# Four attention blocks on one core: a PSUM tile, the order of GpSimd's sums, first loads and products, and the order of the last outputs

## The chip, the cores and the metric

The kernel runs on one core of a Trainium2 chip. The metric is the device time of one execution in microseconds, the median of several runs. In the profile PE is TensorE (matmuls), PEld its weight loads, DVE VectorE, ACT ScalarE, POOL GpSimd, and SP the engine whose queue issues all DMAs here. L716 is line 716 of the kernel before.

## The reference

Four images, `x` of shape (4, 512, 32, 32) in float32, go through four layers, each of which adds its result to `x`. Seen as 512 channels by 1024 positions:

```python
# layer 0: attention, 8 heads of 64
attn = softmax(q @ k.T * 64**-0.5);  x = attn @ v @ Wo.T + bo + x
# layer 1: linear attention with softplus features of 64, and a gate
V = (max(x) + mean(x)) * (wv @ x + bv);  KV = softplus(K) @ V.T
x = x + gamma * (softplus(Q) @ KV) / (softplus(Q) @ sum(softplus(K)))
# layer 2: layer norm over channels, attention with one head of 512
x = x + (softmax(q @ k.T * 512**-0.5) @ v) @ w_proj.T + b_proj
# layer 3: group norm (32 groups), attention, 4 heads of 128
x = x + proj(softmax(q @ k.T * 128**-0.5) @ v)
```

In layers 0, 2 and 3 q, k and v are products of the (normed) input with one weight matrix.

## The kernel before

Everything is in float32. A product of 512 columns goes to PE as two matmul instructions of 0.43 us each, one of 256 columns as two of 0.216.

**Seven products instead of eight.** A product of a 2 by 2 block matrix of weights with a 2 by 2 block matrix of inputs is done with seven block products rather than eight (a Strassen scheme in Winograd's form): in `seven_products` for the projections and the scores of layer 2, in `project_out` for the output projections, in `one_head` for the values of layer 2. Each needs four sums of weight blocks and four of input blocks. `sum_weights` (L702) makes the weight sums on POOL: s[0] (L704), s[1] from s[0] (L705), s[2] (L706), s[3] from s[1] (L707). `sum_inputs` (L692) makes the input sums on DVE. The products are called p1 to p7: p6 takes s[1], p7 s[2], p5 s[0], p3 s[3]. In `seven_products` p1 and p2 of a pair of blocks come first, which need no sums, then p6, p7, p6, p5, p4, p7, p3, p5, p4, p3.

**Order.** PE's order is the order in which the program traces its matmuls (`manual_schedule` for PE). On the other engines a scheduler orders the whole program when it is compiled: among the instructions whose operands it believes to be ready it prefers the one traced earlier. `tc.issue_after(i)` puts what its block traces on i's engine behind i on that engine; it is an order, not a wait. All engines then run in order.

**Where the sums are traced.** In layers 0 and 3 `project_qkv` (L871) calls `seven_products` for four blocks of q and k, with one `sum_weights` each through `block_sums`, then `project_v` (L853), which makes its own four sums once for both of its blocks (L857) into a tile `ws`. In layer 2 the loop over the images b = 0 to 3 traces, in this order: `seven_products` for q with two `sum_weights` (L801); `sum_weights(places, ...)` of the finished q, in the profile `qs`, for the scores (L815); `project_v` with its sums of `hv` (in the profile `ws<-w`, L831 and L857); `one_head` (L832), whose scores take the sums of q. `hv` is made before the loop, q in each turn of it.

**Output projections.** `project_out` (L1071) adds seven products to `x` for one half of the positions (`qb`) of an image in layers 0 and 3. It returns three parts, `second`, `third` and `fourth`, that are called later from the list `later`: after some turns of the attention loop, or all at once. Its first product p1 goes to a PSUM tile ps[1], ACT copies it to `d` (L1112), and `second` adds the second product to the same PSUM tile (`start=False`). `acc_tile` has four buffers in all, for these and for the values and the row sums of attention. The last half of the last image is projected by `end_program` (L1135) without the scheme: three of four chunks of each of four outputs, then `end()` (the verdict: a check whether the fast path held, which ends in `count`), then the last chunk of outputs 0, 2, 1, 3. Outputs 0 and 1 share a PSUM tile, and so do 2 and 3. `finish` (L1065) adds each on DVE and stores it.

**Start.** SP's queue loads chunk by chunk the first half of the positions of image 0 and the q weights (L587, L588), then the k weights (L591), the second half of `x` (L592), the v weights (L593). The first `seven_products` (`first=True`) runs p1 and p2 chunk by chunk for all four blocks, then takes the sums: DVE's need the second half of `x`, POOL's the k weights and the q weights.

## Time and profile before

| what | time |
|---|---|
| median of 3 runs | 2415.14 us (2414.91 to 2416.72) |
| the profiled execution, its own time | 2416.26 us |
| its span, first to last instruction | 2414.5 us |
| PE busy | 2398.0 us, 99% |
| DVE, ACT, POOL busy | 1503.3, 702.0 and 247.8 us |
| share of the chain that ended last | PE 97%, DVE 2% |

Where the four layers lie in the span, read from the groups by line: layer 0 with layer 1 interleaved from the start to about 960 us, layer 2 to 1566 us, layer 3 from there. A row of a timeline gives start and duration, engine, line, operation, output<-inputs, shape and count, and in brackets how long the engine was idle before and what ended that. A row of waits gives the engine and what it made, what it waited for, the total in us, the times and the longest.

### The profile page before, as it was taken

The numbers are of one execution on the slowest core, as the hardware profiler recorded it, in microseconds if no ns is written. First come the engines' busy times: TensorE is split into PE (matmuls) and PEld (weight loads), VectorE is DVE, ScalarE is ACT, GpSimd is POOL, SyncE is SP. The second block draws the span as 40 slices with busy tenths as digits, with TensorE's granted clock in tenths as the row PEclk, the third lists the DMA queues.
The fourth block names the chain that finished last, engine by engine and source line by source line (L and its number), as shares of the span: only waits on it lengthen the run. The fifth ranks groups of instructions, "written<-read, shape, count | busy, mean of one in ns | idle before, by whom it ended". The sixth has DMA issues, their size and how long they took to land.

```text
span 2414.5 us, 24620 instructions
## 1 busy us (share of the span) xinstructions
PE 2398.0 (99%) x10002; PEld 1197.7 (50%) x10002; DVE 1503.3 (62%) x1820; ACT 702.0 (29%) x866; POOL 247.8 (10%) x240
## 2 busy tenths in 40 slices
PE   9999999999999999999999999999999999999999
PEld 4544534453445344544646445455556446455653
DVE  4578577757875789695676765654463554445344
ACT  1454154415531653230302202013221330331132
POOL 4001100110020001102102020111020001002000
PEclk9999999999999999999999999999999999999999
DMA  5001220212021213112001020110010001001001
GB/s 188 2 18 36 57 80 11 61 31 80 19 62 64 99 37 104 64 54 78 1 9 70 13 87 0 61 70 18 35 70 0 23 31 53 0 35 35 0 26 41
DMA packets 44485, 110.15 MB, mean 46 GB/s; under 512 B 3687, under 2 KB 19559, under 8 KB 41422
## 3 DMA queue, kind: packets, MB, share of 16 engines
q1 hardware_dynamic: 44366, 108.52, 13.4%
q8 instruction: 80, 1.31, 0.2%
q14 instruction: 39, 0.32, 0.0%
HBM read 73.69 MB, written 33.77 MB: 45 GB/s over the span
## 4 chain that ended last, share of the span: by engine, by line
PE 97%; DVE 2%; ACT 0%; issue 0%; DMA 0%; SPq 0%; DVEq 0%; ACTq 0%
PE acc L716 19%; PE acc L841 12%; PE acc L976 9%; PE acc L991 9%; PE sc L945 9%; PE sc L940 9%; PE acc L1299 8%; PE acc L848 8%; PE acc L1093 7%; PE acc L1027 1%; PE upd L1534 1%; PE acc L1465 1%; PE feat L1389 0%; PE out L1141 0%; PE feat L650 0%; PE kv L1514 0%
## 5 line engine op out<-in xcount | busy, mean ns | idle before, releaser
L950 ACT ACTIVATE pt<-sc 128x1024 f32<-128x1024 f32 x384 | 379.6, 1022 | 531.6 <-PE sc L945 304.1
L959 DVE TENSOR_TENSOR sum<-sum,pt 128x1024 f32<-128x1024 f32 x256 | 314.5, 1229 | 159.6 <-ACT pt L950 147.0
L976 PE MATMUL acc<-pt,v 64*64 64x512 f32 x2048 | 245.7, 591 | 0.0
L940 PE MATMUL sc<-q,k 64*64 64x512 f32 x2048 | 243.8, 591 | 1.1 <-ACT pt L950 1.1
L991 PE MATMUL acc<-pt,v 128*128 128x512 f32 x512 | 240.8, 594 | 0.0
L945 PE MATMUL sc<-q,k 128*128 128x512 f32 x512 | 239.8, 593 | 0.0
L716 PE MATMUL acc<-t,ws 128*128 128x512 f32 x384 | 173.9, 593 | 0.0
L704 POOL TENSOR_TENSOR ws<-wqkv 128x256 f32<-128x256 f32 (+1 forms) x40 | 39.3, 982 | 1294.2 <-PE acc L1027 513.3
L956 DVE TENSOR_TENSOR sum<-pt 128x1024 f32<-128x1024 f32 x64 | 78.0, 1219 | 137.4 <-ACT pt L950 137.4
L991 PEld LDWEIGHTS acc<-pt,v 128*128 128x128 f32 x512 | 96.6, 190 | 125.3 <-issue 121.6
L945 PEld LDWEIGHTS sc<-q,k 128*128 128x128 f32 x512 | 96.8, 190 | 116.2 <-issue 92.9
L976 PEld LDWEIGHTS acc<-pt,v 64*64 64x64 f32 x2048 | 76.7, 133 | 144.0 <-issue 141.2
L940 PEld LDWEIGHTS sc<-q,k 64*64 64x64 f32 x2048 | 76.3, 133 | 141.8 <-issue 133.0
L716 PEld LDWEIGHTS acc<-t,ws 128*128 128x128 f32 x384 | 72.7, 190 | 88.0 <-issue 87.5
L755 ACT COPY v<-acc 128x512 f32<-128x512 f32 x24 | 14.1, 586 | 305.1 <-PE acc L841 305.1
L687 DVE RECIPROCAL rd<-acc 128x512 f32<-128x512 f32 (+1 forms) x25 | 83.8, 3353 | 29.1 <-PE acc L1027 29.1
L1093 PE MATMUL acc<-ot,wo 128*128 128x256 f32 x360 | 86.7, 383 | 4.1 <-ACT ou L1112 3.4
L755 ACT COPY q<-acc 128x512 f32<-128x512 f32 x40 | 23.5, 586 | 223.6 <-PE acc L716 223.6
L841 PE MATMUL acc<-ws,t 128*128 128x256 f32 x384 | 87.1, 380 | 0.0
L848 PE MATMUL acc<-qs,w 128*128 128x512 f32 x192 | 86.5, 592 | 0.0
L848 PE MATMUL acc<-q,ln 128*128 128x512 f32 x192 | 86.4, 593 | 0.0
L1093 PEld LDWEIGHTS acc<-ot,wo 128*128 128x128 f32 x360 | 67.2, 190 | 28.8 <-issue 10.3
(307 smaller groups left out, 3375.6 us busy)
## 6 DMA issues: line engine op xcount, KB each, us to landing
home<-x SPq DMA_DIRECT2D x8, 2048.0 KB
x<-home SPq DMA_DIRECT2D x8, 2048.0 KB
rds<-quotients SPq DMA_DIRECT2D x32, 256.0 KB
squares<-squares SPq DMA_DIRECT2D x32, 256.0 KB
out<-x SPq DMA_DIRECT2D x32, 256.0 KB
rds<-quotients SPq DMA_DIRECT2D x7, 1024.0 KB
x<-in_x SPq DMA_DIRECT2D x3, 2048.0 KB
v<-squares SPq DMA_DIRECT2D x12, 512.0 KB
```

The lines of the kernel that those rows point to most:

```text
L687: nc.vector.reciprocal(rd, ps)
L716: nc.tensor.matmul(ps, lhsT=w[:, m, :], rhs=x[:, m, :], start=start, stop=stop, skip_group_check=True)
L841: nc.tensor.matmul(ps[:, bass.ts(r, C // 2)], lhsT=x[:, m, bass.ts(2 * o + r, P)], rhs=w[:, m, :], start=(start and r == 0), stop=stop, sk ...
L848: nc.tensor.matmul(ps, lhsT=x[:, m, bass.ts(o, P)], rhs=w[:, m, :], start=start, stop=stop, skip_group_check=True,)
L940: nc.tensor.matmul(ps[half(h), s, :], lhsT=key(g, i)[half(s), half(h)], rhs=q[qb][half(s), g, :], start=True, stop=True,)
L945: nc.tensor.matmul(ps[:, s, :], lhsT=key(g, 2 * i + s), rhs=q[qb][:, g, :], start=True, stop=True)
L950: exps.append(nc.scalar.activation(pt, ps, AF.Exp, scale=scale).ins)
L959: adds.append(nc.vector.tensor_tensor(acc, acc, pt, ALU.add).ins)
L976: nc.tensor.matmul(outs[qb, g][r][half(s), :], lhsT=v[i // 2][half(r), i % 2, g * P + s * hd : g * P + (s + 1) * hd], rhs=pt[half(r), s, : ...
L991: nc.tensor.matmul(outs[qb, g][0], lhsT=v[j // 2][:, j % 2, bass.ts(g, P)], rhs=pt[:, s, :], start=(j == 0), stop=(j == NT - 1),)
L1093: nc.tensor.matmul(ps[i][:, bass.ts(o, n)], lhsT=w[:, m, bass.ts(o, P)], rhs=t[:, m, :], start=(start and m + o == 0), stop=(stop and m == ...
L1299: nc.tensor.matmul(ps[i, o], lhsT=w[m][:, bass.ts(o, P)], rhs=t[m], start=(start and m == 0), stop=(stop and m == 3), skip_group_check=True,)
```

## The change

The loads of the first chunk are split and reordered, six products of `ones` with itself go to PE ahead of everything (their result is read by nothing), `sum_weights` gets an order, the second product in `project_out` gets a PSUM tile, and `end_program` another order; its last output is added and stored in two halves.

```diff
         nc.sync.dma_start(xs[0][:, c, :TB], xin[0, :, c, :TB])
-        nc.sync.dma_start(wqkv0[:, c, :C], wview[:, c, :C])
+        for o in ((0, P), (P, C)) if c == 0 else ((0, C),):
+            nc.sync.dma_start(wqkv0[:, c, slice(*o)], wview[:, c, slice(*o)])
     cols = const.tile([P, NCOLS], F32, name="cols")
     nc.sync.dma_start(cols, d["cols"])
-    nc.sync.dma_start(wqkv0[:, :, C : 2 * C], wview[:, :, C : 2 * C])
     nc.sync.dma_start(xs[0][:, :, TB:], xin[0, :, :, TB:])
+    for o in ((C, C + 2 * P), (C + 2 * P, 2 * C)):
+        nc.sync.dma_start(wqkv0[:, :, slice(*o)], wview[:, :, slice(*o)])
     nc.sync.dma_start(wqkv0[:, :, 2 * C :], wview[:, :, 2 * C :])
...
+    seconds = []
...
     def sum_weights(s, w):
-        nc.gpsimd.tensor_tensor(s[0], w(1, 0), w(1, 1), ALU.add)
-        nc.gpsimd.tensor_tensor(s[1], s[0], w(0, 0), ALU.subtract)
-        nc.gpsimd.tensor_tensor(s[2], w(0, 0), w(1, 0), ALU.subtract)
+        with tc.issue_after(seconds[-1]) if seconds else nullcontext():
+            nc.gpsimd.tensor_tensor(s[0], w(1, 0), w(1, 1), ALU.add)
+        seconds[:] = [nc.gpsimd.tensor_tensor(s[1], s[0], w(0, 0), ALU.subtract).ins]
+        with tc.issue_after(seconds[0]):
+            nc.gpsimd.tensor_tensor(s[2], w(0, 0), w(1, 0), ALU.subtract)
         nc.gpsimd.tensor_tensor(s[3], w(0, 1), s[1], ALU.subtract)
         return s
...
-            mult(1, w(0, 0), inputs(0, 0), stop=False)
+            mult(1, w(0, 0), inputs(0, 0))
             nc.scalar.copy(d, view(ps[1]))
             sum_inputs(t, inputs)
             def second():
-                mult(1, w(0, 1), inputs(1, 0), start=False)
-                finish(0, 0, 1, xv(0, 0))
+                mult(2, w(0, 1), inputs(1, 0))
+                finish(0, 0, 2, xv(0, 0), d)
                 mult(6, os[1], t[1])
                 add(6, d)
...
             two = [two_tile("out") for _ in range(NC // 2)]
-            for o in range(NC):
-                for c in range(NC - 1):
+            def mult(o, cs):
+                ps = two[o // 2][:, o % 2, :]
+                for c in cs:
                     nc.tensor.matmul(
-                        two[o // 2][:, o % 2, :], lhsT=wo[:, c, bass.ts(o, P)], rhs=ot[:, c, :],
-                        start=(c == 0), stop=False,
+                        ps, lhsT=wo[:, c, bass.ts(o, P)], rhs=ot[:, c, :],
+                        start=(c == 0), stop=(c == NC - 1),
                     )
+                if c < NC - 1:
+                    return
+                n = 2 if o == NC - 1 else 1
+                for h in range(n):
+                    ts = bass.ts(h, TB // n)
+                    xv = x[:, o, qb * TB : (qb + 1) * TB][:, ts]
+                    nc.vector.tensor_tensor(xv, ps[:, ts], xv, ALU.add)
+                    nc.sync.dma_start(xout[b, :, o, qb * TB : (qb + 1) * TB][:, ts], xv)
+            early, late = range(NC - 1), (NC - 1,)
+            mult(0, early)
+            mult(2, early)
             end()
-            for o in sorted(range(NC), key=lambda o: o % 2):
-                ps = two[o // 2][:, o % 2, :]
-                nc.tensor.matmul(
-                    ps, lhsT=wo[:, NC - 1, bass.ts(o, P)], rhs=ot[:, NC - 1, :],
-                    start=False, stop=True,
-                )
-                finish(qb, o, ps)
+            mult(0, late)
+            mult(2, late)
+            mult(1, range(NC))
+            mult(3, range(NC))
...
     with tc.manual_schedule(engines={mybir.EngineType.PE}):
+        ps = acc_tile()
+        for _ in range(6):
+            nc.tensor.matmul(ps[:, :P], lhsT=ones, rhs=ones, start=True, stop=True)
```

`finish` of `attention` (L1065) goes, since only `end_program` called it. With `finish(0, 0, 2, xv(0, 0), d)` DVE adds first ps[2], then `d` to `x`, where one addition of ps[1] stood before.

## The prediction

> **What bounds the kernel now.** I read the shares of the page first, then TensorE's own waits, then the stages around each edit.

> ```profile
> PE 2398.0 (99%) x10002; PEld 1197.7 (50%) x10002; DVE 1503.3 (62%) x1820; ACT 702.0 (29%) x866; POOL 247.8 (10%) x240
> ```

> TensorE (PE) has work for all but 16.5 us of the 2414.5 us span. The change takes no product away, so it can win only from those 16.5 us and from slow matmuls, and anything that makes PE wait costs its full length. The waits of PE, in total, times and longest:

> ```profile
> PE acc L716 <- DMA wqkv<-in_wqkv: 4.7, 1, 4.7
> PE acc L1093 <- ACT ou L1112: 3.4, 5, 0.7
> PE sc L940 <- ACT pt L950: 1.1, 4, 0.3
> PE acc L1093 <- DVE ot L1060: 0.7, 1, 0.7
> ...
> ```

> The change aims at the first two rows. GpSimd (POOL) is no releaser in this list: its sums are always ready before PE asks. With 10% busy that looks like plenty of room, so I checked where its order has slack. In layer 2, image 1, its timeline is:

> ```profile
> 1124.22 1.72 POOL L704 TENSOR_TENSOR ws<-w 128x512 f32<-128x512 f32 x1
> 1125.90 1.26 POOL L706 TENSOR_TENSOR ws<-w 128x512 f32<-128x512 f32 x1
> 1127.12 1.27 POOL L705 TENSOR_TENSOR ws<-ws,w 128x512 f32<-128x512 f32 x1
> 1128.46 1.27 POOL L707 TENSOR_TENSOR ws<-w,ws 128x512 f32<-128x512 f32 x1
> 1146.66 2.35 POOL L704 TENSOR_TENSOR qs<-q 128x1024 f32<-128x1024 f32 x1 [16.93 <-DVE q L748]
> 1148.96 2.35 POOL L706 TENSOR_TENSOR qs<-q,q 128x1024 f32<-128x1024 f32 x1
> 1151.27 2.35 POOL L705 TENSOR_TENSOR qs<-qs,q 128x1024 f32<-128x1024 f32 x1
> 1153.70 2.38 POOL L707 TENSOR_TENSOR q<-q,qs 128x1024 f32<-128x1024 f32 x1
> ```

> The first four are the weight sums of project_v (traced at L857), the last four the sums of q for one_head (traced at L815, so earlier in the program). POOL runs the later-traced ones first, 17 us before q exists. PE at the same place:

> ```profile
> 1145.63 7.07 PE L841 MATMUL acc<-w,ln 128*128 128x256 f32 x32
> 1152.53 1.02 PE L1580 MATMUL lnsums<-s,ones 128*128 128x512 f32 x2
> 1153.39 2.97 PE L841 MATMUL acc<-ws,w 128*128 128x256 f32 x13
> ```

> At 1153.39 p6 of project_v takes ws, namely s[1], the sum of L705. It was ready at 1128.4: 25 us of slack, all of it owed to POOL's order.

> **The change, part by part.**

> *Sums in order.* Each s[0] now goes to POOL behind s[1] of the sum_weights call traced before it; s[2] behind its own s[1]. For project_v of layer 2 the call before is L815, so ws cannot start until q is complete and two q sums have run. The rows give the price. q is complete at 1146.66 (DVE q L748). After s[1] of q, POOL may take s[2] of q or s[0] of ws; the order of before shows that the earlier-traced ready one goes first (L706 ahead of L705, which was still waiting for L704's result), so I take all four q sums first: 1146.66 + 4 x 2.35 + 0.1 = 1156.2. Then s[0] and s[1] of ws: 2 x 1.27 + 0.1 = 2.6, so 1158.8. PE wants it at 1153.39: a stall of 5.4. Image 2 is the same (q sums from 1295.61, PE at 1302.34, 1295.61 + 12.1 - 1302.34 = 5.4). Image 3: q sums from 1444.56, PE at 1450.66: 6.0. Image 0, where pieces of the linear attention fill PE: 985.41 + 12.1 - 996.74 = 0.8. Sum 17.6; restarts add 0.1 each (320 against 216 ns between the first two matmuls after a wait at L1093): **+18.0**. s[2] follows 1.3 later and p7 wants it 1.7 later, so nothing more stalls there; the q sums are needed only in one_head, after 1170. Behind the waiting p6 every later matmul is queued, and PE has no slack to win it back. Bounds: +4 if only the two q sums that the edge demands go first (1146.66 + 4.7 + 2.6 = 1153.95 for images 1 and 2, 1451.9 for image 3: 0.6, 0.6, 1.2, plus restarts and one collision of 0.5 each with DVE); +21.6 if both sums of ws collide with DVE in every image (1.72 for 1.27 in the row of 1124.22: 8 x 0.45 more).

> In layers 0 and 3 the same edge puts project_v's sums behind the third and fourth block's; there they end near 265, and p6 of project_v comes after 281: covered by 16 us. Cost nothing.

> *The clock after a stall.* The start shows what an idle PE does:

> ```profile
> 8.24 0.34 PEld L716 LDWEIGHTS acc<-x,wqkv 128*128 128x128 f32 x1 [0.52 <-issue]
> 9.10 0.34 PEld L716 LDWEIGHTS acc<-x,wqkv 128*128 128x128 f32 x1 [0.52 <-issue]
> 9.88 0.19 PEld L716 LDWEIGHTS acc<-x,wqkv 128*128 128x128 f32 x1 [0.45 <-issue]
> 10.31 0.19 PEld L716 LDWEIGHTS acc<-x,wqkv 128*128 128x128 f32 x1 [0.24 <-issue]
> ```

> Weight loads are 0.85 apart until 9.88, then 0.43: from 4.70 on PE ran at half speed for 5.2 us and lost 2.6. At the end, by windows (PE to ACT to POOL busy, then granted clock, DMA):

> ```profile
> 2411.00:2413.00 2.00, 0.00 (x0) 0.00 (x0) 0.00 (x0) 0.00 (x0) 0.00 (x0) 0.94 0.11 35
> 2413.00:2414.40 1.40, 0.00 (x0) 0.00 (x0) 0.00 (x0) 0.00 (x0) 0.00 (x0) 0.50 0.03 6
> ```

> a mean of 0.94 puts the fall to 0.50 at 2412.76, 4.3 us after PE's last matmul (2408.5). Three stalls of 5.4 to 6.0 are longer than that. Each such fall costs up to 2.6, as at the start. Bounds: 0 (none falls) to 7.8 (all three); I take two: **+5.2**.

> [...]

> *Second product in its own PSUM tile.* Now PE waits at L1093 for ACT to copy ps[1] (L1112) before it adds to it. Starts of the matmuls around the wait at 1714.01: 1055 and 320 ns where 216 is the pace, so 0.94 lost. It is 5 times: four in layer 3 (1714, 1924, 2134, 2344) and one at 920. The four go: **-3.8**. The copy's next reader is DVE's add of d, 1.7 us later: not late. The new tile is a fifth allocation where four buffers turn: ps[1] comes free after ACT's copy instead of after DVE's add, and ps[6] and ps[7] start behind 1.7 us products, so I find no new wait for a buffer. At 920 nothing is won: PE stops there again at 922.12 for ot (DVE L1060), whatever went before. Each call also has one more DVE add (x += d, 0.69); in attention DVE is idle beside it (gaps of 1 us between its adds at 1717 to 1721). Near 930 it isn't: from 925 to 965 DVE is busy 39.81 of 40 us, and PE waits for it at 966.39. There it costs **+0.7** (0 if the scheduler finds a gap).

> *Loads and first products.* The first chunk of weights comes in 64 KB and 192 KB. By the landing events x was there at 3.91 and the 256 KB of weights at 4.56; a quarter of 0.65 is 0.16, and smaller packets are slower, so the first real matmul starts at 4.3: -0.4 (0 to -0.5). The six products of ones need only DVE's memset (over at 1.07) and take 12 x 0.214 = 2.6 us at half speed (0.85 for 512 columns, a quarter for 128), until 4.0: they delay nothing, and if they count as work, the clock rises 5.2 after them instead of after 4.70, so at 1.2 + 5.2 = 6.4. From 4.3 to 6.4 half of 2.1 is lost instead of 2.6: -1.6 (bounds 0 and -2.6). With x ahead of the k weights DVE's four input sums start at 12.9 instead of 15.6; POOL's sums start at 14.4 instead of 12.9 and run one for each DVE sum (1.70 instead of 0.72, as at 16.3 to 21.4), so that s[1] of block 1 is ready at 21.5; PE then wants it at about 22.4 (24.5 before, less 2.0). Covered by 1 us; with all 2.6 won it would give 0.5 back. Together **-2.0**.

> *Last outputs.* Before: 24 matmuls early, then 8 with two small waits, 14.33 us from 2394.17. After: 12 early (5.15, so until 2399.3; ot is ready at 2398.0, the verdict's row at 2398.5: covered by 0.8), then 20 at 0.43 and one wait of 0.2 for DVE's add of output 0: 14.1. The last DVE add is cut in two, the second half ends 0.1 later; its DMA is smaller, but the span ends through DVE's and PE's branch (PE's takes 3.97). **-0.2** (+0.2 to -0.6).

> **Sum.** +18.0 + 5.2 - 3.8 + 0.7 - 2.0 - 0.2 = +17.9. The profiled execution took 2416.26 (span 2414.5 and 1.8 around it), which gives 2434.2. It stands 1.1 above the median of the runs, 2415.14, and the three runs spread over 1.8, which a different moment of the first clock rise can do. Made against the median the sum is 2433.0; a median run that rose earlier has less to win at the start, but a mean of two falls of the clock is also the less certain term. I take **2432.5**.

> **Rivals.**

> *The clock stays up.* Stall as above, no falls: 2433.0 - 5.2 = 2427.8. For it: the fall at the end needed 4.3 us, so stalls of 5.4 are only just long enough. It lies in my range.

> *A short stall.* POOL takes s[0] of ws after s[1] of q, with s[2] of q between it and s[1] of ws (not ready at once): 1146.66 + 3 x 2.35 + 0.1 + 2 x 1.27 = 1156.3, stalls of 2.9, 2.9, 3.5, below the 4.3 of the clock. With restarts +9.6: 2415.14 + 9.6 - 5.3 = 2419.4. Against it: in the groups of before that I read the traced order wins among ready sums.

> *The chain does not bite* (the other side). If project_v's sums still run ahead of q, because the edge leads elsewhere than I read, the first term and the clock's are nothing and the four waits and the start decide: 2415.14 - 3.8 + 0.7 - 2.0 - 0.2 = 2409.8. It decides as soon as s[1] of ws ends before 1153.4. Against it: `seconds` is one list for all calls, and L815 stands between the calls of L801 and L857.

> **How the numbers follow.** A measurement of this kernel tells 0.2% (4.8 us) from no change. Forecast 0.86 (with its no-fall variant, about 0.3 of it), short stall 0.06, no bite 0.08. Forecast and falls span 2433.0 - 5.2 - 3 = 2425 to 2433.0 + 2.6 + 2 = 2438; the lower end goes to 2423 for a fuller gain at the start (1.6 more), the upper holds a third fall (2.6) and half of the collisions (2). So 2423 to 2438. Faster takes about half of the last rival, since 2409.8 lies at 0.2%: 0.05. Same: the rest of it and half of the short stall: 0.06. Slower: 0.89.

> **What would show it.** Right: a row of PE waiting for POOL ws L705 (none before), about 18 in 4 times, with ws sums after the qs sums on POOL; PEld rows 0.85 apart behind some of these waits; no wait for ou L1112 in layer 3; first real matmul near 4.3. Wrong: ws sums ahead of qs sums, or PE's wait on POOL under 5 us in total; then the time is near 2410.

## The result and the profile after

The changed kernel takes **2434.12 us** (median of 4 runs, 2431.77 to 2435.99) where the kernel before takes 2415.15: a ratio of 1.0076, 95% interval 1.0064 to 1.0089. That is 19 us slower. Its profiled execution has a span of 2433.0 us, 18.5 more than before.

The shares of the page, the same line as before:

```profile
PE 2407.7 (99%) x10014; PEld 1205.5 (50%) x10014; DVE 1506.5 (62%) x1836; ACT 701.4 (29%) x866; POOL 241.7 (10%) x240
```

PE is still 99% busy, and its busy time has grown by 9.7 us although only twelve short instructions were added. Matmuls at half clock last longer (32 of them 9.87 us instead of 7.07, below) and count as busy, so a share says nothing here. The waits of PE, with their totals, times and longest, do:

```profile
PE acc L850 <- POOL ws L713: 16.1, 4, 5.6
PE acc L1096 <- DVE ot L1069: 1.7, 1, 1.7
PE sc L949 <- ACT pt L959: 1.1, 4, 0.3
PE acc L1694 <- DVE ones L629: 1.1, 1, 1.1
```

The waits for `wqkv` (4.7) and for ACT's copies (3.4 in 5 times) are gone, as the change wants. In their place stands one for POOL, 16.1 us in four waits, one for each image of layer 2. L850 is the matmul of `project_v` (L841 before) and L713 is s[1] (L705 before). POOL's timeline at image 1 of layer 2:

```profile
1145.36 2.34 POOL L712 TENSOR_TENSOR qs<-q 128x1024 f32<-128x1024 f32 x1 [21.74 <-DVE q L757]
1147.78 2.35 POOL L713 TENSOR_TENSOR qs<-qs,q 128x1024 f32<-128x1024 f32 x1
1150.08 2.35 POOL L715 TENSOR_TENSOR qs<-q,q 128x1024 f32<-128x1024 f32 x1
1152.39 1.27 POOL L712 TENSOR_TENSOR ws<-w 128x512 f32<-128x512 f32 x1
1153.61 2.36 POOL L716 TENSOR_TENSOR q<-q,qs 128x1024 f32<-128x1024 f32 x1
1155.92 1.26 POOL L713 TENSOR_TENSOR ws<-ws,w 128x512 f32<-128x512 f32 x1
```

POOL sits idle for 21.7 us until q is there, where before it summed the weights of `ws` from 1124 on; then it does all four sums of q ahead of s[1] of `ws` (ended 1157.18). PE at the same place:

```profile
1151.23 1.02 PE L1596 MATMUL lnsums<-s,ones 128*128 128x512 f32 x2
1157.24 9.87 PE L850 MATMUL acc<-ws,w 128*128 128x256 f32 x32 [4.99 <-POOL ws L713]
```

The 32 matmuls behind the wait take 9.87 us; undisturbed they take 7.07. The granted clock tells why: the same stretch cut at the clock's edges, with busy us of PE, PEld, DVE, ACT and POOL, then the granted clock, the busy share of DMA and its GB/s.

```profile
1152.50:1155.91 3.41, 0.00 (x0) 0.00 (x0) 1.68 (x3) 1.87 (x3) 3.41 (x2) 1.00 0.01 2
1155.91:1159.32 3.41, 2.08 (x5) 1.71 (x6) 0.00 (x0) 0.00 (x0) 3.41 (x4) 0.50 0.00 0
1159.32:1162.74 3.42, 3.42 (x9) 2.67 (x9) 1.61 (x3) 0.00 (x0) 0.31 (x1) 0.50 0.00 0
1162.74:1166.15 3.41, 3.41 (x17) 3.00 (x17) 2.62 (x5) 1.91 (x2) 0.00 (x0) 1.00 0.00 0
```

PE was idle through 1152.50 to 1155.91, and at the end of that stretch the clock fell to 0.50 and stayed there for two stretches of 3.41. Images 2 and 3 look the same: PE was idle through 1309.51 to 1312.92 and 1466.52 to 1469.94, and the clock was at 0.50 until 1319.75 and 1476.76.

To see where the 18.5 went, compare the starts of the same matmuls in both profiles, one after another; where the distance changes, time was lost or won. The places, in us:

| place | step |
|---|---|
| first product that takes a sum (21.04 before, 18.87 after) | -2.17 |
| from there to 930: a wait for POOL at 22.6 (+0.43), a later sum of DVE at 671 (+0.36), +0.17 at 927 | +0.96 |
| 930 to 977, PE behind DVE | -0.67 |
| `project_v` in layer 2, wait for `ws`, images 0 to 3 | +0.58 +5.15 +5.16 +5.77 |
| half clock behind it, images 1 to 3 | +2.80 +2.85 +2.89 |
| the four output projections of layer 3 | 4 x -0.94 |
| from the start of the last output's addition on DVE to the end (5.9 to 4.9) | -1.0 |

The sum is +18.6 by these rounded steps; the spans differ by 18.5.

### The profile page after: what moved, and what is told of

It reads as the page before. It is cut to its first block, busy times and chain, and to the rows that moved or that the text cites. A ratio compares the mean times of both kernels' runs of the same rounds, so it can differ in the third digit from the quotient of the medians.

```text
span 2433.0 us, 24713 instructions
## 1 busy us (share of the span) xinstructions
PE 2407.7 (99%) x10014; PEld 1205.5 (50%) x10014; DVE 1506.5 (62%) x1836; ACT 701.4 (29%) x866; POOL 241.7 (10%) x240
## 3 DMA queue, kind: packets, MB, share of 16 engines
q8 instruction: 81, 1.33, 0.2%
## 5 line engine op out<-in xcount | busy, mean ns | idle before, releaser
L850 PE MATMUL acc<-ws,t 128*128 128x256 f32 x384 | 87.1, 380 | 0.0
L857 PE MATMUL acc<-qs,w 128*128 128x512 f32 x192 | 86.5, 592 | 0.0
L857 PE MATMUL acc<-q,ln 128*128 128x512 f32 x192 | 86.4, 593 | 0.0
L1096 PE MATMUL acc<-oi,os 128*128 128x256 f32 x360 | 81.3, 380 | 0.2 <-DVE oi L702 0.2
```

The costliest lines, as they stand in the source:

```text
L850: nc.tensor.matmul(ps[:, bass.ts(r, C // 2)], lhsT=x[:, m, bass.ts(2 * o + r, P)], rhs=w[:, m, :], start=(start and r == 0), stop=stop, sk ...
L857: nc.tensor.matmul(ps, lhsT=x[:, m, bass.ts(o, P)], rhs=w[:, m, :], start=start, stop=stop, skip_group_check=True,)
L1096: nc.tensor.matmul(ps[i][:, bass.ts(o, n)], lhsT=w[:, m, bass.ts(o, P)], rhs=t[:, m, :], start=(start and m + o == 0), stop=(stop and m == ...
```

## The experiments

### The order alone, and the change without it

The order between calls of `sum_weights` is one `with` statement. It is taken out (`no_chain`), both orders are taken out (`no_order`), the order between calls is put alone into the kernel before (`chain_only`), and, with the orders kept, the weight sums of `project_v` are traced ahead of those of q (`ws_first`).

```diff
# no_chain, against after (no_order also drops the one before s[2])
-        with tc.issue_after(seconds[-1]) if seconds else nullcontext():
-            nc.gpsimd.tensor_tensor(s[0], w(1, 0), w(1, 1), ALU.add)
+        nc.gpsimd.tensor_tensor(s[0], w(1, 0), w(1, 1), ALU.add)
# ws_first, against after
+            wsv = sums_v(hv, wpool.tile([P, NC, C], F32, tag="wo", name="ws"))
             sum_weights(places, lambda i, j: pair(q[i], j))
...
-            project_v(vt, hv, normed(xn), made, wpool.tile([P, NC, C], F32, tag="wo", name="ws"))
+            project_v(vt, hv, normed(xn), made, None, wsv)
```

`sums_v` makes the four sums that `project_v` made itself.

> The changed kernel without the order between calls (s[0] of a call no longer behind s[1] of the call before); the order inside a call stays. Theory (project_v's sums of layer 2 wait behind q's, and TensorE falls to half speed in the stalls): the 16.7 us of stalls and 8.5 us of half speed go, 2434.1 - 25.2 = 2408.9, no row of PE waiting for POOL ws of more than 1 us, granted clock 1.0 throughout. Rival (the loss sits in the order inside a call, the PSUM tile or the extra DVE add): above 2425.

> The changed kernel without either order on GpSimd. Theory: like the last, 2409 to 2410; at the start block 1 gets its s[1] after s[2], up to 0.7 later than with the order inside a call. If the order inside a call cost anything, this is below the last by more than 1.

> The changed kernel with its full order, but in layer 2 project_v's sums are traced ahead of the sums of q. Theory: the chain then follows the order in which the operands get ready, 2408.9, as without the chain. Rival (any order between calls costs, wherever it leads): above 2415.

> The kernel before with the order between calls alone. Theory: 2415.1 + 16.7 + 8.5 = 2440.3, PE waits for POOL ws 4 times, half speed behind three of them. Rival (the stall comes only together with the other edits): within 2 of 2415.

| kernel | median us | ratio to before |
|---|---|---|
| `no_chain` | 2411.37 | 0.9981 (0.9972 to 0.9990) |
| `no_order` | 2411.93 | 0.9983 (0.9974 to 0.9992) |
| `ws_first` | 2410.50 | 0.9977 (0.9968 to 0.9987) |
| `chain_only` | 2439.33 | 1.0098 (1.0082 to 1.0113) |

(before, on the same chip: 2416.18). One statement decides: without it the rest of the change is a gain of 0.2%, alone it loses 23 us. The first waits of `chain_only`:

```profile
PE acc L844 <- POOL ws L708: 15.7, 4, 5.5
PE acc L719 <- DMA wqkv<-in_wqkv: 4.8, 1, 4.8
PE acc L1096 <- ACT ou L1115: 3.4, 5, 0.7
```

The new wait stands beside both old ones. In `ws_first`, which has exactly the same orders, POOL's timeline of image 1 is:

```profile
1122.90 1.71 POOL L712 TENSOR_TENSOR ws<-w 128x512 f32<-128x512 f32 x1
1124.69 1.26 POOL L713 TENSOR_TENSOR ws<-ws,w 128x512 f32<-128x512 f32 x1
1125.91 1.26 POOL L715 TENSOR_TENSOR ws<-w 128x512 f32<-128x512 f32 x1
1127.13 1.27 POOL L716 TENSOR_TENSOR ws<-w,ws 128x512 f32<-128x512 f32 x1
1145.22 2.35 POOL L712 TENSOR_TENSOR qs<-q 128x1024 f32<-128x1024 f32 x1 [16.82 <-DVE q L757]
```

So it is not an order as such that costs, but this order over a trace in which sums that are ready late stand ahead of sums that are ready early. At the start the order gives PE a little: in the profiles `no_order` has a wait of PE for POOL's sums of 1.2 us, `no_chain` one of 0.4, `ws_first` none. That the whole kernel gains by it is not shown: the three times lie within 1.5 us of each other, and their intervals overlap; the profile of `no_order` also shows half speed from 922.78 (24 matmuls take 7.10 us, in `ws_first_again` 5.42).

### The half clock, apart from the stall

In `fill` PE gets 20 products of `ones` ahead of p6 in images 1 to 3 of layer 2. They add nothing to the output and fill the stall without shortening it. In `three_first` the fourth sum of q is moved behind s[1] of `ws`, which shortens the stall by one q sum.

```diff
# fill
+        ahead()
         for a in range(0, n, 2):
...
+            def fill():
+                ps = acc_tile() if b else None
+                for _ in range(20 if b else 0):
+                    nc.tensor.matmul(ps[:, :P], lhsT=ones, rhs=ones, start=True, stop=True)
# three_first
-            sum_weights(places, lambda i, j: pair(q[i], j))
+            sum_weights(places, lambda i, j: pair(q[i], j), False)
...
+            with tc.issue_after(seconds[0]):
+                nc.gpsimd.tensor_tensor(places[3], pair(q[0], 1), places[1], ALU.subtract)
```

> The changed kernel with 20 products of ones (40 matmuls of 128 columns, 4.3 us) on TensorE just ahead of p6 of project_v, in images 1 to 3 of layer 2; they add nothing to the output. The stalls stay, but TensorE is idle for under 1.5 us in each. Theory (the half speed behind the stalls comes from idling): the clock stays at 1.0 and the 8.5 us of half speed go, 2434.1 - 8.5 = 2425.6, while the start of p6 does not move. Rival (the half speed has another cause, or the fillers delay p6): 2434 or more.

> The changed kernel with s[3] of q put behind s[1] of project_v's sums, so that three and not four q sums stand ahead. Theory: stalls of 5.15 - 2.35 + 0.1 = 2.9, 2.9 and 3.5 and none in image 0; 7.4 us of stall go, and if stalls of this length leave the clock alone, 8.5 more: 2434.1 - 15.9 = 2418.2. Rival (half speed follows shorter idling too): some 2427, clock at 0.5 behind the stalls.

`fill` took 2426.62 us, ratio 1.0047 (1.0032 to 1.0063) to the 2415.41 of before. Its clock stays up behind the stalls (1.00 from 1152.50 to 1159.30 at image 1, a mean of 0.999 over the span). PE at image 1:

```profile
1151.08 4.63 PE L1858 MATMUL acc<-ones 128*128 128x128 f32 x40
1156.72 7.17 PE L851 MATMUL acc<-ws,w 128*128 128x256 f32 x32 [1.01 <-POOL ws L713]
```

The stall is not shorter: p6 is delayed by 0.49, 0.50 and 0.03 us more than in the changed kernel; in image 1 POOL's s[1] takes 1.72 here where it took 1.26. But the 32 matmuls behind it take 7.17 instead of 9.87. Compared matmul by matmul, the half clock of the three images cost 8.2 us that are now gone: its price, apart from the stall. The two profiled spans differ by 8.3 (1.0 lost by the longer stalls, 1.0 won before layer 2), the medians by 7.5.

`three_first` took 2425.52 us, ratio 1.0040 (1.0024 to 1.0055): the theory's time was missed by 7 us, near the rival. The stalls were what the theory says (p6 later by 2.98, 2.99 and 3.61), but the clock followed two of the shorter stalls as well, which cost 3.1 and 1.8 us. Another 1.7 of the 7 has nothing to do with them: in the profile there is also half speed from 921.59, behind the wait for `ot` (24 matmuls take 7.10 us, in `ws_first_again` 5.42). Images 1 and 2, again cut at the clock's grid:

```profile
1153.70:1157.11 3.41, 1.52 (x7) 1.37 (x8) 0.99 (x2) 1.70 (x3) 3.33 (x4) 1.00 0.01 2
1157.11:1160.53 3.42, 3.42 (x18) 3.01 (x17) 2.84 (x3) 0.00 (x0) 3.19 (x2) 1.00 0.00 0
1303.88:1307.30 3.42, 1.33 (x5) 0.45 (x3) 1.89 (x3) 1.88 (x4) 3.34 (x3) 1.00 0.00 0
1307.30:1310.71 3.41, 2.67 (x6) 2.19 (x7) 0.00 (x0) 0.56 (x1) 3.41 (x4) 0.50 0.00 0
1310.71:1314.12 3.41, 3.41 (x9) 2.70 (x8) 1.89 (x3) 0.27 (x1) 2.04 (x1) 0.50 0.00 0
```

In image 1 PE was busy for 1.52 of 3.41 and the clock held; in image 2 it was busy for 1.33, and the clock fell for two stretches. In image 3 the 1.8 fit one stretch.

### The PSUM tile and the end, each alone

`psum_only` is the kernel before with the second product in its own PSUM tile; `end_only` is the kernel before with the new `end_program`.

```diff
# psum_only, against before
-            mult(1, w(0, 0), inputs(0, 0), stop=False)
+            mult(1, w(0, 0), inputs(0, 0))
...
-                mult(1, w(0, 1), inputs(1, 0), start=False)
-                finish(0, 0, 1, xv(0, 0))
+                mult(2, w(0, 1), inputs(1, 0))
+                finish(0, 0, 2, xv(0, 0), d)
```

> The kernel before with the second product in a PSUM tile of its own and its extra DVE add, nothing else. By the prediction: 4 waits of 0.94 in layer 3 go, 0.7 comes near 966: 3.1 below the kernel before. By the trace of the changed kernel (no loss near 966): 3.8 to 4.3 below. Rival (the gain of these waits is given back later): within 1.

> The kernel before with the last outputs in the new order and the last one in halves, nothing else. By the prediction 0.2 less, by the trace of the changed kernel 1.0 less, because the span ends 4.9 instead of 5.9 after the start of the last DVE add.

`psum_only`: 2413.22 us, ratio 0.9990 (0.9981 to 0.9999): 2.2 under the 2415.4 of before, short of the theory's 3.1 and beyond the rival's 1. The waits for ACT are gone, but the other one of `project_out` has grown:

```profile
PE acc L716 <- DMA wqkv<-in_wqkv: 4.2, 1, 4.2
PE acc L1093 <- DVE ot L1060: 1.7, 1, 1.7
```

At 920 us PE needs `ot` from DVE anyway; it now arrives there sooner and waits once for 1.7 instead of twice for 0.7. Nothing is won or lost at that place, but the pieces of idling have become one. In layer 3 all four steps of -0.94 appear, and near 960 us a loss of 0.55: 0.38 at 951 and 0.16 at 966.

`end_only`: 2414.95 us, ratio 0.9997 (0.9988 to 1.0006), which the measurement doesn't tell from no change. In its profile the span ends 5.0 us after the start of the last DVE addition instead of 5.9.

### The start, and the loss near 966 us, on the best order

The last four were measured together: `ws_first` again, and it without the products of ones, with the loads as before the change, and with the old accumulation in ps[1] in the last half of image 3 of layer 0.

```diff
# ws_first_no_ones
-        for _ in range(6):
-            nc.tensor.matmul(ps[:, :P], lhsT=ones, rhs=ones, start=True, stop=True)
# ws_first_one_old
+            own = not (pair and b == B - 1 and qb == NTB - 1)
+            mult(1, w(0, 0), inputs(0, 0), stop=own)
...
+                else:
+                    mult(1, w(0, 1), inputs(1, 0), start=False)
+                    finish(0, 0, 1, xv(0, 0))
# ws_first_old_loads
-        for o in ((0, P), (P, C)) if c == 0 else ((0, C),):
-            nc.sync.dma_start(wqkv0[:, c, slice(*o)], wview[:, c, slice(*o)])
+        nc.sync.dma_start(wqkv0[:, c, :C], wview[:, c, :C])
...
+    nc.sync.dma_start(wqkv0[:, :, C : 2 * C], wview[:, :, C : 2 * C])
...
-    for o in ((C, C + 2 * P), (C + 2 * P, 2 * C)):
-        nc.sync.dma_start(wqkv0[:, :, slice(*o)], wview[:, :, slice(*o)])
```

> The kernel after, its orders of sums all kept, with the weight sums of project_v traced ahead of the sums of q in layer 2: the earlier run of this order, now in five rounds and beside three variants of it. Theory (the loss was only the place of project_v's sums behind those of q): about 2410.5 us, 0.998 of the kernel before, no wait of TensorE on POOL in layer 2. Rival (the gain seen before was the moment of a clock rise in those runs): within 0.1% of before.

> The same order without the six products of ones at the start (they add nothing to the output). Theory (these products count as work for the clock and raise it sooner): the rise comes one step of 3.41 us later in part of the runs, and the time is 1.0 to 2.5 us above that of the same order with them, about 2412. Rival (the rise is set by the real products alone, or TensorE waits there for x and weights anyway): no difference beyond 0.5 us.

> The same order, but in layer 0, image 3, last half, the second product of the output projection is added up in the first one's PSUM tile, as before the change. Theory (there the extra addition on VectorE, busy without a gap from 925 to 965, costs 0.5 us at the product that waits for w): 0.5 us less, about 2410, with the start of that product moved by 0.1 at most against before beyond the shift of the start; it is less than five rounds tell apart, so the profile decides. Rival (VectorE's addition is hidden there, and the 0.5 is another wait): the same step of 0.5 in the profile.

> The same order with the loads as before the change (first chunk of weights in one piece, k weights ahead of the rest of x). Theory (the smaller first piece is what lets the first product start early): first product at about 4.7 instead of 3.9, input sums of VectorE from 15.6 instead of 14.0, and the first product that takes a sum about 0.5 to 1.5 us later; time 2411 to 2412. Rival (the products of ones and the clock are all of the gain at the start): the first product that takes a sum starts within 0.3 us of the same order with the new loads, time within 0.5 us.

| kernel | median us (range) | ratio to before |
|---|---|---|
| `ws_first_again` | 2409.98 (2409.17 to 2411.53) | 0.9976 (0.9966 to 0.9985) |
| `ws_first_no_ones` | 2411.58 (2410.47 to 2411.83) | 0.9982 (0.9973 to 0.9991) |
| `ws_first_one_old` | 2409.81 (2409.19 to 2410.26) | 0.9975 (0.9965 to 0.9985) |
| `ws_first_old_loads` | 2410.68 (2409.75 to 2412.29) | 0.9979 (0.9970 to 0.9988) |

`ws_first` holds: 0.24% under before, faster than both kernels. **The ones.** Without them the time is 1.6 us more, inside the expected 1.0 to 2.5, though the two intervals overlap. The timelines of PE, first with and then without them:

```profile
1.12 2.93 PE L1698 MATMUL acc<-ones 128*128 128x128 f32 x12 [1.12 <-DVE ones L629]
3.84 1.22 PE L725 MATMUL acc<-x,wqkv 128*128 128x512 f32 x2
5.66 13.14 PE L725 MATMUL acc<-x,wqkv 128*128 128x512 f32 x30 [0.60 <-DMA wqkv<-in_wqkv]
```

```profile
3.81 15.49 PE L725 MATMUL acc<-x,wqkv 128*128 128x512 f32 x32 [3.81 <-DMA wqkv<-in_wqkv]
19.14 5.31 PE L725 MATMUL acc<-t,ws 128*128 128x512 f32 x12
```

In the first the clock rose at 4.21 (the two products at 3.84 take 1.22, at full clock 1.02), in the second at 6.87 (the 32 from 3.81 take 15.49, at the full pace of 0.43 13.9): products that nobody reads did count as work here, since PE had run little else by 4.21. But at full speed PE overtakes the weights and waits for them at 5.66, so of the 1.5 us that the half clock costs in the second (half of 6.87 - 3.81) only 0.3 is won at the first product that takes a sum (18.84 against 19.14). And that 0.3 does not last: with the ones, PE waits for POOL's sums again at 22.7, and from 23.2 on the kernel without them is 0.2 ahead. The profiled spans differ by 1.2 all the same, because in the second the clock falls at 921.65, worth 1.7, and in the first it does not. So the gain at the start is not what the 1.6 shows. Whether the ones had a hand in that, through the moment at which the grid lies, is open. **The loads.** With the old ones the first real matmul starts at 4.52 instead of 3.84, the product with a sum 0.3 later, and the time is 0.7 more with overlapping intervals: the theory's half to 1.5 us at that product was missed, the rival's 0.3 met, though not its 0.5 in the time. In the profiles the 0.3 is lost again in the same way, and both spans are 2408.5, so where the 0.7 comes from is not shown.

**The loss near 966.** It is still 0.52 with the old accumulation, so the added DVE instruction is not its cause here. What is, the timelines of POOL and DVE show. In `ws_first_one_old`:

```profile
953.89 1.27 POOL L712 TENSOR_TENSOR ws<-w 128x512 f32<-128x512 f32 x1 [12.92 <-ACT w L1797]
954.14 1.04 DVE L563 TENSOR_TENSOR bo<-bo,cols 128x4 f32<-128x4 f32 x1
```

and before:

```profile
956.83 1.29 POOL L704 TENSOR_TENSOR ws<-w 128x512 f32<-128x512 f32 x1
956.93 0.10 DVE L563 TENSOR_TENSOR bo<-bo,cols 128x4 f32<-128x4 f32 x1
```

An addition of four columns took 0.10 before and 1.04 here: it ended at 955.18, and POOL's sum at 955.16. DVE has hardly a gap from there to the `w` that PE waits for; it had come to the addition 0.5 us sooner against PE than before, so 0.5 of the delay is left, and PE's wait for `w` grows from 0.28 to 0.80.

In `psum_only` the same addition takes 1.11, but DVE's four instructions behind it (`ln`) take 3.80 there instead of 4.74, so the meeting explains about 0.1 of the 0.55. The 0.38 at 951 comes ahead of POOL's sums: PE waits there for DVE's `sq`, which is 0.31 us earlier than before where PE is 0.75 earlier. That fits one more DVE instruction of some 0.6 us on a DVE without gaps, but it was not tested alone.

## Why the prediction was right

The forecast was 2432.5 (2423 to 2438), and 2434.12 came out, by the mechanism that it named. That the sum came so close is in part luck: the clock cost 3.3 us more than reckoned and the start gave 0.8 less, while the stall (1.3), the place near 930 (1.4) and the end (0.8) made up for it.

**The stall** was put at +18.0 and took +16.7, with 0.58, 5.15, 5.16 and 5.77 for 0.8, 5.4, 5.4 and 6.0. The order within POOL was slightly off: s[0] of `ws` ran ahead of the fourth sum of q, not behind it. That changes nothing, since s[1] of `ws` came behind all four in any case. The size is off by little because the six sums took 11.8 us (1145.36 to 1157.18) where 12.1 was reckoned: consecutive rows of POOL overlap by some 0.05, which the working added rather than took away.

**The clock** is the step that was mis-sized: two falls of 2.6, +5.2, where three of 2.80 to 2.89 came, +8.5. The prediction had one fall to go by, at the end, 4.3 us after PE's last matmul; that two of three stalls would bring one was its author's estimate, and so was the loss at the start (2.6) as the most that one costs. `three_first` shows that less idling was enough: a fall came behind a stretch of 3.42 in which PE was busy for 1.33 and idle for 2.09. A stall that leaves PE idle for 5.0 us, laid anywhere on a grid of 3.41, fills at least 2.5 of one stretch, more than those 2.09. So, as an estimate from that fall, all three would have come wherever the grid lay; only shorter stalls, as in `three_first`, leave it to the moment. For the same reason the rival of a short stall was priced too low: 2419.4 forecast, 2425.5 measured for its stalls of 3.0 to 3.6 (1.7 of the 6.1 is the fall at 921, which the stalls did not make). The rival in which the clock stays up, 2427.8, is what `fill` made by hand, 2426.6.

**The PSUM tile** gave -3.8 as forecast. The +0.7 near 930 to 966 for the added DVE instruction is what failed in this part: the place gave -0.67. Alone, in `psum_only`, the tile did lose 0.55, of which 0.38 fits the added instruction; with `ws_first` the loss there is 0.52, with the addition of four columns beside POOL's sums of layer 2 (0.59 us for 0.10). In the changed kernel those sums are held back behind q, so POOL is silent there, DVE's four instructions `ln` take 2.70 us instead of 4.74, and the place at 966 won 0.4 instead (-0.4 also in `chain_only`, `fill` and `three_first`).

**The start** was put at -2.0 and came to -2.17, less a wait of 0.43 that the prediction had covered by a margin of 1 us: the input sums of DVE started at 14.01, not 12.9, and with them POOL's. Another 0.36 went at 671, where PE waits for a sum of DVE. The first real matmul came at 3.87, where 4.3 was forecast; the forecast called smaller packets slower, and in the trace of before those of 512 B took a mean of 60 ns, those of 2048 B 112. **The end** was put at -0.2 and came to -1.0. The prediction had the matmuls 0.2 shorter and the end of the span set by the branches of DVE and PE. Neither shows: from the last 32 matmuls' first start to their end it is 14.48 us in both kernels, and PE's branch (3.97 us from 2408.17 before, 4.18 from 2422.56 after) ended at 2412.14 and 2426.74, ahead of the last store's landing both times. That store was issued at 2409.31 and landed at 2412.78 before; after, with half the bytes, it was issued at 2429.03 and landed at 2431.56. So 0.9 of the 1.0 is its landing, 2.5 us after the issue instead of 3.5 (2.2 in `end_only`). Whether the smaller store or the other order of the last outputs does that was not tested apart.

**The chain that does not bite**, 2409.8, is the kernel with the two calls exchanged: 2410.0. The price was right, again with errors that cancel (the end gave 0.8 more, the start 0.8 less than reckoned in the changed kernel), and nothing spoke for the case itself.

## What to carry to other kernels

An order laid on an engine that runs in order is an order of readiness too (here POOL sat idle for 21.7 us in front of sums of `ws` that `ws_first` runs at 1122.90): before chaining calls as they are traced, list when each operand is ready, and where a later-traced call was ready sooner, its old slack is the first thing to price. Where such an edge is wanted, exchange the calls and the same edge is harmless. And a stall of TensorE should be priced with the clock behind it: here 8.5 us on 16.7 of stall. In `chain_only` PE waits 15.7 us for `ws`, and behind the wait of image 1 the 32 matmuls take 9.14 us instead of 7.07. The least idling of PE within one stretch of the grid that a fall is seen to follow was 1.84 us (`ws_first_no_ones`).

## What was not expected of the hardware

**When the clock fell and rose.** In the trace of the changed kernel the granted clock changes at 5.62, 1155.91, 1162.74, 1312.92, 1319.75, 1469.94, 1476.76 and 2432.49: these times are 337, 2, 44, 2, 44, 2 and 280 steps of 3.413 us apart. In the trace of before it changes at 9.80 and 2412.78, 704 such steps apart. Counted from the start of the span the steps lie at 2.20 in the one and at 2.97 in the other. Stretches of this grid at full clock, by how long PE was busy in them:

| run | stretch | PE busy of 3.41 or 3.42 | clock behind it |
|---|---|---|---|
| changed kernel | 1152.50, 1309.51, 1466.52 | 0.00 | 0.50 |
| `three_first` | 1303.88 | 1.33 | 0.50 |
| `three_first` | 1153.70 | 1.52 | 1.00 |
| `ws_first_no_ones` | 918.23 | 1.58 | 0.50 |
| `ws_first_old_loads` | 917.51 | 1.75 | 1.00 |
| changed kernel | 916.98 | 2.10 | 1.00 |

The ends of matmuls are modelled, so 1.52 and 1.58 are not told apart. Two neighbours, from `ws_first_no_ones` and `ws_first_old_loads`:

```profile
918.23:921.65 3.42, 1.58 (x7) 0.84 (x6) 3.03 (x6) 1.76 (x4) 0.00 (x0) 1.00 0.03 5
921.65:925.06 3.41, 3.41 (x9) 2.70 (x10) 3.33 (x6) 0.00 (x0) 0.00 (x0) 0.50 0.90 250
```

```profile
917.51:920.93 3.42, 1.75 (x8) 1.23 (x7) 3.03 (x6) 2.26 (x4) 0.00 (x0) 1.00 0.00 0
920.93:924.34 3.41, 3.25 (x15) 2.57 (x15) 3.41 (x7) 0.00 (x0) 0.00 (x0) 1.00 0.75 206
```

**An addition of DVE beside a running sum of POOL.** In `psum_only`, `ws_first`, `ws_first_again` and `ws_first_one_old` the addition of four columns began 0.17 to 0.70 us after the start of a POOL sum and ended 0.01 to 0.03 us after that sum's end, taking 1.11, 0.59, 0.59 and 1.04 us instead of 0.10. Before and in `end_only`, where it began 0.10 us after the start of the POOL sum, it took 0.10.
